# Layer 3's cross attention: the softmax weights of all heads side by side, transposed and multiplied in blocks of 128 keys

## The chip, the cores and the metric

The kernel runs on one core of a Trainium2 chip. A core has five engines that each work through a queue of their own and meet at semaphores: PE (TensorE, matrix products and transposes; PEld is its loading of weights), DVE (VectorE), ACT (ScalarE), POOL (GpSimd) and SP (SyncE, which issues most transfers). The metric is the device time of one execution in microseconds, as the median of several. All data are 32-bit floats.

## The reference

A decoder of four layers works on `x` of shape (4, 512, 128): four batches of 512 tokens of width 128. Each layer adds self attention, cross attention on a context of 77 rows, and a feed-forward. The change is in Layer 3's cross attention, which has 16 heads of 64:

```python
q = (query @ w_q).reshape(B, Q, HEADS, HEAD_DIM).transpose(0, 2, 1, 3)
k = (key @ w_k).reshape(B, Kl, HEADS, HEAD_DIM).transpose(0, 2, 1, 3)
v = (value @ w_v).reshape(B, Kl, HEADS, HEAD_DIM).transpose(0, 2, 1, 3)
scores = jnp.einsum('bhqd,bhkd->bhqk', q, k) * scale
attn = jax.nn.softmax(scores, axis=-1)
out = jnp.einsum('bhqk,bhkd->bhqd', attn, v)
out = out.transpose(0, 2, 1, 3).reshape(B, Q, HEADS * HEAD_DIM)
return out @ w_o
...
x = x + _L3_xattn_ref(_layernorm(x, axis=-1), ctx_1024, ctx_1024, L3_xattn_w_q, L3_xattn_w_k, L3_xattn_w_v, L3_xattn_w_o)
x = x + _L3_ffn_ref(_layernorm(x, axis=-1), L3_ffn_gate_w, L3_ffn_bias, L3_ffn_W1, L3_ffn_W3, L3_ffn_W2, L3_ffn_sw1, L3_ffn_sw3, L3_ffn_sw2)
```

Layer 3's feed-forward, which follows, is a mixture of 32 experts: each token goes to four of them, and each expert has a limited number of places (slots).

## The kernel before, in words

*Tiles.* P = 128 partitions, B = 4 batches, S = 512 tokens a batch, TB = 4 tiles of 128 tokens a batch, D = 128, L = 77 context rows. `xT` holds the normalised tokens as columns, `x` and `xn` hold them as rows.

*Keys and values ahead of time.* `l3_context` (woven into Layer 0's feed-forward) computes the keys of all heads and, for each head, the product of its values with its part of the output matrix: `vo` of head h has 77 rows of width 128, so that the sum over heads of weights times `vo` is already the attention's output. Both go to memory (L1999, L2012). `l3_keys` (L2015 to L2024) loads them into `kb` and `vo` ahead of Layer 3; `kb` has the two heads of a pair in a block diagonal form, so that one product gives the scores of both.

*The stage.* `l3_xattn` (L2026 to L2086) makes 32 items, four batches of eight pairs of heads, and runs four phases of each, shifted against each other: in round r stand the projection of item r, the scores of item r - 1, the products with the values of item r - 4 and the transposes of item r - 3.
- Projection: one product 128 by 512 (L417) into a bank of PSUM, copied with the scale 1/8 into `q` by ACT (L2042).
- Scores: four products (L417), two token tiles in each of two banks `s`. Then for each bank: DVE takes the maximum of each row (L516) and subtracts it into a tile `sm_e` of 4 x 77 columns (L428), ACT takes the exponential (L2059), DVE the sums and their reciprocals (L525, L526), POOL multiplies (L527). So an item has two sets of these, each 128 x 308.
- Transposes: for each of the two heads four transposes (L2068, `mm<-ident,sm_e`) of 128 tokens by 77 keys, and a copy by ACT to `eT` (L2070).
- Values: for each head one product over 77 keys (L2077, `acc<-eT,vo`) that adds into the batch's accumulator, 16 in a batch; after the last, ACT copies it to `yT` (L2083).

PSUM has eight banks: five for `mm` (projection, scores and transposes), two accumulators `acc` and one `s` for everything in the chain below.

*What is woven in.* The first 12 rounds carry the layer norms of batches 1 to 3. Rounds 12 to 19 carry a chain for batch 0, the next eight rounds one for batch 1, the remaining rounds one for batch 2, each about two and a half pieces a round. Such a chain adds the attention's output of its batch to `x` (four transposes L448 of `yT`, DVE's add L428), takes the layer norm (L475 to L508: statistics and the iterated root on DVE, the scaled rows on ACT, four transposes L507 on PE) and routes the batch (`route_slots`): gate products on PE, the four best experts by DVE (L620 to L640), the "place" products of L417 (how many tokens went to the same expert before), then `fits` (L706) and the slot numbers `to` (L737) on DVE, and last 16 scatters of 128 rows each, issued by POOL (L749). The batch's scatters need `to`; the experts need the scatters of batches 0 to 2. Batch 3 goes through a dense feed-forward later.

The program text gives the order in which the work is issued; the framework's scheduler arranges each engine's queue from it, so neighbours may change places on an engine, but each engine then works strictly through its queue. The multiplies (L527) of POOL and its scatters (L749) share one queue, as do the softmax passes and the routing on DVE.

*After the stage.* Shared rows, the experts on their slots, the gathers of their results (L860) and the dense feed-forward of batch 3 end the kernel; they have weights that POOL loads (L369).

Of the kernel before, what the change touches and what calls it, by code (L numbers as in the profile page):

```python
# [13 lines left out]
F32 = mybir.dt.float32  # L14
# [4 lines left out]
ALU = mybir.AluOpType  # L19
AX = mybir.AxisListType  # L20
PSUM = bass.MemoryType.PSUM

P = 128
B, S, D = 4, 512, 128
NT = B * S // P
TB = S // P
L = 77
# [261 lines left out]
class Net:  # L289
# [1694 lines left out]
    def l3_context(self, pool):  # L1984

        nc = self.nc
        Wk, Wv, Wo = (self.load("l3_xattn." + n, pool, "x3" + n) for n in "kvo")
        kd = self.away.tile([2, 64, 8, B, L], F32, name="x3_k")
        vd = self.away.tile([L, 16, B, D], F32, name="x3_vo")
        self.x3 = kd, vd  # L1990
        yield
        for hp in range(8):
            c = slice(hp * P, hp * P + P)
            pk = self.bank("f", (P, B, L))
            self.dot(pk.rearrange("p b l -> p (b l)"), (Wk["k"][:, c], self.const["ctxT"]))
            k = pool.tile([P, B, L], F32, tag="x3kT", name="x3kT", bufs=2)
            nc.scalar.copy(k, pk)
            for h in range(2):
                nc.sync.dma_start(kd[h, :, hp], k[64 * h : 64 * h + 64])  # L1999
            pv = self.bank("f", (P, B * L))  # L2000
            self.dot(pv, (Wv["v"][:, c], self.const["ctxT"]))
            vT = pool.tile([P, B * L], F32, tag="x3vT", name="x3vT", bufs=2)
            nc.scalar.copy(vT, pv)
            yield
            vo = pool.tile([L, 2, B, D], F32, tag="x3vo", name="x3vo", bufs=2)
            for h in range(2):
                po = self.bank("f", (P, B, D))
                r = slice(64 * h, 64 * h + 64)
                for b in range(B):
                    self.dot(po[:L, b, :], (vT[r, b * L : b * L + L], Wo["o"][r, c]))  # L2010
                nc.scalar.copy(vo[:, h], po[:L])
            nc.sync.dma_start(vd[:, 2 * hp : 2 * hp + 2], vo)  # L2012
            yield

    def l3_keys(self, pool):  # L2015

        kd, vd = self.x3
        kb = pool.tile([P, 8, B, 2, L], F32, name="kb")
        vo = pool.tile([L, 16, B, D], F32, name="vo")
        self.nc.gpsimd.memset(kb, 0.0)  # L2020
        for h in range(2):
            self.nc.sync.dma_start(kb[64 * h : 64 * h + 64, :, :, h, :], kd[h])
        self.nc.sync.dma_start(vo, vd)
        self.x3 = kb, vo  # L2024

    def l3_xattn(self, base, pool):  # L2026


        nc, tc = self.nc, self.tc
        HP = 8  # L2030
        Wq = self.pack(base, "l3_xattn.q")
        kb, vo = self.x3
        items = [(b, hp) for b in range(B) for hp in range(HP)]
        made = {}
        accs = {}

        def projections(b, hp):
            c = slice(hp * P, hp * P + P)
            pq = self.mm()
            self.dot(pq, (Wq["q"][:, c], self.tokens(b)))  # L2040
            q = pool.tile([P, S], F32, tag="q", name="q", bufs=3)
            nc.scalar.mul(q, pq, 0.125)  # L2042
            made[b, hp, "q"] = q

        def scores(b, hp):
            q = made.pop((b, hp, "q"))
            es = []
            for j0 in range(0, TB, 2):
                s = self.mm((P, 4, L))
                for j in range(2):  # L2050
                    self.dot(
                        s[:, 2 * j : 2 * j + 2, :].rearrange("p h l -> p (h l)"),
                        (q[:, (j0 + j) * P : (j0 + j + 1) * P], kb[:, hp, b].rearrange("p h l -> p (h l)")),
                    )
                es.append(s)
            made[b, hp, "e"] = []
            for s in es:
                e = self.less_maxima(s, 4, pool, 8)
                nc.scalar.activation(e, e, AF.Exp)  # L2059
                self.over_sums(e, 4, pool, 8)  # L2060
                made[b, hp, "e"].append(e)

        def turn(b, hp):
            es = made.pop((b, hp, "e"))
            for h in range(2):
                t = self.mm((P, TB, P))
                for j in range(TB):
                    nc.tensor.transpose(t[:L, j, :], es[j // 2][:, 2 * (j % 2) + h, :], self.ident)  # L2068
                eT = pool.tile([L, S], F32, tag="eT", name="eT", bufs=4)
                nc.scalar.copy(eT, t[:L].rearrange("l j q -> l (j q)"))  # L2070
                made[b, hp, h] = eT

        def values(b, hp):
            if hp == 0:
                accs[b] = self.acc()
            for h in range(2):
                nc.tensor.matmul(  # L2077
                    accs[b], lhsT=vo[:, 2 * hp + h, b, :], rhs=made.pop((b, hp, h)),
                    start=hp == 0 and h == 0, stop=hp == HP - 1 and h == 1,
                )  # L2080
            if hp == HP - 1:
                self.sums["l3_xattn", b] = pool.tile([P, S], F32, tag="yT", name="yT", bufs=2)
                nc.scalar.copy(self.sums["l3_xattn", b], accs[b])  # L2083

        return self.lagged(items, (projections, 0), (scores, 1), (values, 4), (turn, 3))

    def out(self, b):
# [206 lines left out]
```

## Time and profile before

| | |
|---|---|
| time, five runs | 2347.26, 2352.25, 2352.82, 2356.02, 2359.11 us; median 2352.82 |
| profiled execution | 2365.31 us, its span 2363.5 us |
| PE busy | 2205.5 us, 93% of the span |
| DVE, ACT, POOL busy | 1605.9 (68%), 1034.3 (44%), 571.7 us (24%) |
| first projection of the stage, last value product | near 2032 and near 2205 us |
| first scatter of batch 0, 1, 2 | 2115.55, 2160.98, 2203.32 us |
| transposes L2068, 256 of them | mean 280 ns |
| value products L2077, 128 passes | mean 594 ns |
| softmax passes on DVE, 64 sets: L516, L428, L525, L526 | mean 471, 468, 469, 171 ns |
| multiplies L527 on POOL, 64 in the stage | mean 706 ns |

The span is the time between the first and the last event of the profiled execution. In the profile's rows, L is a line of the kernel, then come the engine, the operation, the tile written and the tiles read, the shape, and how often it ran; then its busy time in us, the mean duration of one in ns, and the engine's idle time just before, with what ended it. A chain of waits is followed back from the last instruction: at each step to what released it, or to the instruction before it on its engine. Instructions overlap in their pipelines, so several of a kind take less than their number times the mean.

### The profile page before, as it was taken

How to read it: one execution, taken by the hardware profiler on the slowest of the kernel's cores; microseconds unless marked ns; L12 is line 12 of the kernel's file. 1: busy time of each engine (PE TensorE's matmuls, PEld its weight loads, DVE VectorE, ACT ScalarE, POOL GpSimd, SP SyncE). 2: the span in 40 equal slices, each digit the busy share in tenths (PEclk: the TensorE clock that was granted, in tenths of full speed). 3: DMA queues.
4: the chain of work that ended last, by engine and by line, in shares of the span. 5: the costliest groups of instructions: out<-in, count | busy, mean ns of one | idle time of the engine just before them, and what ended most of it. 6: DMA issues, size and time to landing. Idle time of an engine off the chain costs nothing.

```text
span 2363.5 us, 28673 instructions
## 1 busy us (share of the span) xinstructions
PE 2205.5 (93%) x9282; PEld 1162.0 (49%) x9282; DVE 1605.9 (68%) x4051; ACT 1034.3 (44%) x2105; POOL 571.7 (24%) x712
## 2 busy tenths in 40 slices
PE   6999899999999998999999999999999995998865
PEld 3566556644545453445444444444444443765532
DVE  6666566666676678778776787767767756776433
ACT  4555446344325553434443444444444433455410
POOL 1000001000000103333323333323333322336343
PEclk7888899999999999999999999999999997999887
DMA  5321144154453242233433334333333350000287
GB/s 160 93 64 42 44 119 123 47 142 113 114 133 94 79 130 76 74 87 94 110 85 83 96 97 109 115 80 93 101 101 91 101 134 36 1 6 1 63 164 75
DMA packets 84144, 210.95 MB, mean 89 GB/s; under 512 B 18873, under 2 KB 41721, under 8 KB 83661
## 3 DMA queue, kind: packets, MB, share of 16 engines
q1 hardware_dynamic: 79050, 198.99, 31.1%
q0 software_dynamic: 4944, 10.14, 3.5%
q8 instruction: 73, 1.20, 0.2%
q14 instruction: 77, 0.63, 0.1%
HBM read 179.76 MB, written 20.23 MB: 85 GB/s over the span
## 4 chain that ended last, share of the span: by engine, by line
PE 73%; DVE 13%; issue 5%; DMA 4%; POOL 3%; ACT 2%; SPq 0%; POOLq 0%; ACTq 0%; DVEq 0%
PE mm L417 21%; PE f L417 11%; PE mm L1783 8%; PE s L417 8%; PE acc L947 5%; PE mm L1750 5%; PE mm L1733 4%; DMA back<-made,back 2%; DVE h L428 2%; PE acc L2077 2%; PE mm L1115 1%; PE mm L1070 1%; PE mm L1137 1%; DVE m L1077 1%; PE s L507 1%
## 5 line engine op out<-in xcount | busy, mean ns | idle before, releaser
L1694 POOL TENSOR_TENSOR gvx<-gvx 128x512 f32<-128x512 f32 (+1 forms) x256 | 259.8, 1015 | 584.1 <-DVE gvx L428 528.4
L417 PE MATMUL f<-xT,w_l_ffn 128*128 128x512 f32 (+1 forms) x768 | 376.0, 611 | 11.3 <-DVE h L428 10.6
L417 PE MATMUL mm<-w_l_ffn_qkv,xT 128*128 128x512 f32 x512 | 266.3, 604 | 3.3 <-DVE roped L1665 1.7
L1814 ACT ACTIVATE at_e<-mm,at_m 128x512 f32<-128x512 f32 x256 | 172.9, 686 | 213.6 <-DVE at_m L1812 207.9
L1783 PE MATMUL mm<-og,w_l_ffn_o 128*128 128x512 f32 x512 | 264.9, 601 | 0.0
L939 ACT ACTIVATE h<-f 128x512 f32<-128x512 f32 x189 | 112.3, 596 | 292.3 <-PE f L417 265.2
L947 PE MATMUL acc<-h,w_l_ffn 128*128 128x512 f32 x378 | 201.1, 617 | 31.1 <-DVE h L428 23.3
L417 PEld LDWEIGHTS f<-xT,w_l_ffn 128*128 128x128 f32 (+1 forms) x768 | 141.6, 194 | 166.8 <-issue 130.5
L428 DVE TENSOR_TENSOR h<-h,f 128x512 f32<-128x512 f32 (+1 forms) x192 | 131.1, 684 | 130.1 <-PE f L417 102.0
L428 DVE TENSOR_TENSOR og<-mm,c 128x512 f32<-128x512 f32 x256 | 175.5, 687 | 27.3 <-PE mm L1783 26.0
L428 DVE TENSOR_TENSOR gvx<-mm,gv 128x512 f32<-128x512 f32 x256 | 174.2, 682 | 23.3 <-PE mm L417 18.9
L1734 ACT COPY eT<-mm 128x512 f32<-128x512 f32 x256 | 137.6, 595 | 73.0 <-PE mm L1733 72.8
L1812 DVE TENSOR_REDUCE at_m<-mm 128x1 f32<-128x512 f32 x256 | 161.0, 682 | 7.8 <-PE mm L417 6.1
L1733 PEld LDWEIGHTS mm<-ident,at_e 128*128 128x128 f32 x1024 | 119.6, 141 | 67.3 <-issue 49.5
L1783 PEld LDWEIGHTS mm<-og,w_l_ffn_o 128*128 128x128 f32 x512 | 89.5, 191 | 97.6 <-issue 86.1
L1733 PE MATMUL mm<-ident,at_e 128*128 128x128 f32 x1024 | 133.5, 273 | 2.6 <-ACT at_e L1814 2.6
L947 PEld LDWEIGHTS acc<-h,w_l_ffn 128*128 128x128 f32 x378 | 71.8, 196 | 126.6 <-issue 73.2
L417 PEld LDWEIGHTS mm<-w_l_ffn_qkv,xT 128*128 128x128 f32 x512 | 86.9, 190 | 92.3 <-issue 70.0
L417 PE MATMUL mm<-roped 64*128 64x512 f32 x512 | 131.7, 616 | 0.5 <-DVE gvx L428 0.4
L1077 DVE TENSOR_REDUCE m<-mm 128x1 f32<-128x512 f32 (+3 forms) x176 | 105.4, 636 | 37.3 <-PE mm L1073 36.5
L428 DVE TENSOR_TENSOR h<-h,c 128x512 f32<-128x512 f32 x176 | 121.2, 695 | 4.1 <-DMA c<-l_ffn_w 1.0
L1750 PE MATMUL mm<-eT,v 128*64 128x512 f32 x512 | 119.9, 600 | 0.0
(440 smaller groups left out, 3688.1 us busy)
## 6 DMA issues: line engine op xcount, KB each, us to landing
c<-gates SPq DMA_DIRECT2D x256, 256.0 KB
c<-l_ffn_w SPq DMA_DIRECT2D x106, 384.0 KB
w_l_ffn<-in_l_ffn SPq DMA_DIRECT2D x26, 576.0 KB
w_l_ffn_qkv<-in_l_ffn_qkv SPq DMA_DIRECT2D x16, 640.0 KB
w_l_ffn_o<-in_l_ffn_o SPq DMA_DIRECT2D x16, 512.0 KB
rot<-qk SPq DMA_DIRECT2D x128, 64.0 KB
w_l_ffn<-in_l_ffn POOLq DMA_DIRECT2D x10, 576.0 KB, 4.4
k_parts<-k SPq DMA_DIRECT2D x12, 384.0 KB
```

The lines of the kernel that those rows point to most:

```text
L417: self.nc.tensor.matmul(out, lhsT=lhsT, rhs=rhs, start=i == 0, stop=i == len(pairs) - 1)
L428: self.nc.vector.tensor_tensor(out, a, b, op)
L939: nc.scalar.activation(h, pg, AF.Silu)
L947: nc.tensor.matmul(acc["t"], lhsT=W["d" + u], rhs=h, start=i == 0, stop=i == n - 1)
L1077: nc.vector.tensor_reduce(m[:, i, h0 : h0 + per], ps, AX.X, ALU.max, negate=True)
L1694: nc.gpsimd.tensor_tensor(x[:, :, :m], x[:, :, :m], x[:, :, m : 2 * m], ALU.add)
L1733: nc.tensor.transpose(p[:, j, :], es[i][hl][:, j * P : j * P + P], self.ident)
L1734: nc.scalar.copy(eT[hl][:, :, i * P : i * P + P], p)
L1750: nc.tensor.matmul(po[64 * hl : 64 * hl + 64, :], lhsT=m["v"][:, j, hl, :], rhs=eT[hl][:, j, :], start=j == 0, stop=j == TB - 1,)
L1783: nc.tensor.matmul(acc, lhsT=W["o"][:, (e - 1) * D : e * D], rhs=hs.pop(e - 1), start=e == 1, stop=e == E)
L1812: nc.vector.tensor_reduce(m, s, AX.X, ALU.max, negate=True)
L1814: nc.scalar.activation(e[:, :n], s, AF.Exp, bias=m, accum_out=den)
```

## The change

The weights of one batch now lie in one tile `heads` of 128 tokens by 4 token tiles by 16 heads by 77 keys, two of them in turn. The subtraction of each set writes its piece (two token tiles, the two heads of the pair: 2 x 154 columns) into that tile, and exponential, sums and multiply work on the same piece. The number and the sizes of these instructions are as before. The 16 x 77 = 1232 keys of all heads are cut into blocks of 128 regardless of heads: nine full ones and one of 80. The transposes and the products with the values go by these blocks: 10 x 4 transposes and 10 products a batch instead of 16 x 4 and 16. A block is taken up with the pair of heads that completes it; the eight pairs of a batch have 1, 1, 1, 1, 2, 1, 1 and 2 blocks. The value tile is laid out to match, 128 rows by 10 blocks: `l3_context` writes its rows of (head, key) one below the other, and `l3_keys` loads nine full blocks and a rest of 80 rows in two transfers.

```diff
-        vd = self.away.tile([L, 16, B, D], F32, name="x3_vo")
+        vd = self.away.tile([16 * L, B, D], F32, name="x3_vo")
...
-            nc.sync.dma_start(vd[:, 2 * hp : 2 * hp + 2], vo)
+            nc.sync.dma_start(vd[2 * hp * L : 2 * (hp + 1) * L].rearrange("(h l) b d -> l h b d", l=L), vo)
...
-        vo = pool.tile([L, 16, B, D], F32, name="vo")
+        n, rest = 16 * L // P, 16 * L % P
+        vo = pool.tile([P, n + 1, B, D], F32, name="vo")
...
-        self.nc.sync.dma_start(vo, vd)
+        self.nc.sync.dma_start(vo[:, :n], vd[: n * P].rearrange("(r p) b d -> p r b d", p=P))
+        self.nc.sync.dma_start(vo[:rest, n], vd[n * P :])
...
+        rows = [(r, min(r + P, 16 * L)) for r in range(0, 16 * L, P)]
+
+        blocks = [[i for i, (_, r) in enumerate(rows) if (r - 1) // (2 * L) == hp] for hp in range(HP)]
...
-            made[b, hp, "e"] = []
-            for s in es:
-                e = self.less_maxima(s, 4, pool, 8)
+            if hp == 0:
+                made[b, "e"] = pool.tile([P, TB, 16, L], F32, tag="heads", name="heads", bufs=2)
+            for i, s in enumerate(es):
+                s = s.rearrange("p (j h) l -> p j h l", j=2)
+                e = made[b, "e"][:, 2 * i : 2 * i + 2, 2 * hp : 2 * hp + 2, :]
+                m, r = (pool.tile([P, 2, 2], F32, tag=t, name=t, bufs=8) for t in ("sm_m", "sm_s"))
+                wide = lambda a: a.unsqueeze(3).to_broadcast([P, 2, 2, L])
+                nc.vector.tensor_reduce(m, s, AX.X, ALU.max)
+                self.tt(e, s, wide(m), ALU.subtract)
                 nc.scalar.activation(e, e, AF.Exp)
-                self.over_sums(e, 4, pool, 8)
-                made[b, hp, "e"].append(e)
+                nc.vector.tensor_reduce(r, e, AX.X, ALU.add)
+                nc.vector.reciprocal(r, r)
+                nc.gpsimd.tensor_tensor(e, e, wide(r), ALU.mult)
 
         def turn(b, hp):
-            es = made.pop((b, hp, "e"))
-            for h in range(2):
+            e = made[b, "e"].rearrange("p j h l -> p j (h l)")
+            for i in blocks[hp]:
+                r0, r1 = rows[i]
                 t = self.mm((P, TB, P))
                 for j in range(TB):
-                    nc.tensor.transpose(t[:L, j, :], es[j // 2][:, 2 * (j % 2) + h, :], self.ident)
-                eT = pool.tile([L, S], F32, tag="eT", name="eT", bufs=4)
-                nc.scalar.copy(eT, t[:L].rearrange("l j q -> l (j q)"))
-                made[b, hp, h] = eT
+                    nc.tensor.transpose(t[: r1 - r0, j, :], e[:, j, r0:r1], self.ident)
+                eT = pool.tile([P, S], F32, tag="eT", name="eT", bufs=4)
+                nc.scalar.copy(eT[: r1 - r0], t[: r1 - r0].rearrange("l j q -> l (j q)"))
+                made[b, i] = eT
 
         def values(b, hp):
             if hp == 0:
                 accs[b] = self.acc()
-            for h in range(2):
+            for i in blocks[hp]:
+                n = rows[i][1] - rows[i][0]
                 nc.tensor.matmul(
-                    accs[b], lhsT=vo[:, 2 * hp + h, b, :], rhs=made.pop((b, hp, h)),
-                    start=hp == 0 and h == 0, stop=hp == HP - 1 and h == 1,
+                    accs[b], lhsT=vo[:n, i, b, :], rhs=made.pop((b, i))[:n], start=i == 0, stop=i == len(rows) - 1,
                 )
```

The scheduler arranges the engines' queues anew for this program, so places of unchanged instructions differ too. A weight load of the experts (L369 on POOL), which overwrites Layer 3's projection weights and so waits for PE's last projection, stood ahead of the multiplies of items 30 and 31 and now stands ahead of those of items 28 to 31. Batch 2's norm transposes (L507) stood after the transposes of item 27 and now stand after those of item 29.

## The prediction

> **What bounds the kernel now.** I first read the chain that ended last: TensorE (PE) holds most of it, and the stage's own lines are the values L2077 and part of L417.
>
> ```profile
> PE 73%; DVE 13%; issue 5%; DMA 4%; POOL 3%; ACT 2%; SPq 0%; POOLq 0%; ACTq 0%; DVEq 0%
> ```
> ```profile
> 2047.95 1.91 PE mm L417 x10
> 2049.86 1.72 PE acc L2077 x4
> 2051.58 0.88 PE mm L2068 x8
> ```
>
> The second block is the chain inside Layer 3's cross attention: a round (one pair of heads) is projection and scores 1.91, values 1.72, transposes 0.88, together 4.50 us with no gap. 32 rounds run from 2032 to 2205 us. But the windows by stage say that this bound does not last:
>
> ```profile
> core 0: us, PE busy (x) PEld busy (x) DVE busy (x) ACT busy (x) POOL busy (x), PEclk, DMA share, GB/s
> 2051.60:2060.60 9.00, 9.00 (x46) 6.04 (x45) 5.59 (x17) 5.01 (x11) 2.71 (x4) 1.00 0.01 3
> ...
> 2079.00:2115.50 36.50, 35.56 (x191) 24.89 (x190) 27.35 (x113) 22.82 (x45) 9.69 (x15) 1.00 0.00 1
> 2115.50:2161.00 45.50, 42.41 (x209) 28.58 (x208) 32.47 (x125) 25.19 (x49) 27.11 (x34) 0.96 0.03 7
> 2161.00:2203.30 42.30, 39.09 (x195) 26.02 (x193) 29.37 (x115) 22.31 (x44) 26.26 (x32) 0.96 0.06 15
> ```
>
> In steady rounds DVE has 2.79 of 4.50 us to do. From 2079 a batch's routing is woven in (27 to 32 us of DVE per batch), and from 2115.5 POOL also issues the 16 scatters of a batch. POOL's timeline shows what they do to the softmax multiplies (L527) that the transposes wait for, and PE's timeline the wait:
>
> ```profile
> 2115.55 1.30 POOL L749 DMA_INDIRECT slots<-xn,to  x1 [3.74 <-DVE to L737]
> ...
> 2137.61 0.97 POOL L749 DMA_INDIRECT slots<-xn,to  x1 [0.30 <-issue]
> 2138.60 3.98 POOL L527 TENSOR_TENSOR sm_e<-sm_e,sm_s 128x308 f32<-128x308 f32 x6
> ```
> ```profile
> 2131.70 0.44 PE L2068 MATMUL mm<-ident,sm_e 128*77 128x128 f32 x2 [1.84 <-POOL sm_e L527]
> 2132.35 1.09 PE L2068 MATMUL mm<-ident,sm_e 128*77 128x128 f32 x6 [0.21 <-POOL sm_e L527]
> 2133.23 1.91 PE L417 MATMUL mm<-xT,w_l_xattn_q 128*128 128x512 f32 x2
> ...
> 2139.37 0.44 PE L2068 MATMUL mm<-ident,sm_e 128*77 128x128 f32 x2 [0.83 <-POOL sm_e L527]
> ```
>
> I call the start of batch b's scatters Sb (S0 2115.55, S1 2160.98, S2 2203.32) and the transposes of item k Tk (T0 2041.5, T8 2079.0, T19 2140.0 and T27 2185.4 where the multiplies come free). After S2 some 160 us follow (experts, gathers, the last dense feed-forward) that the change does not touch. So the end moves as S2 moves.
>
> **The change, part by part.** The rows:
>
> ```profile
> L527 POOL TENSOR_TENSOR sm_e<-sm_e,sm_s 128x308 f32<-128x308 f32 x64 | 43.8, 706 | 70.1 <-DVE sm_s L526 38.7 <-PE mm L417 18.3 <-ACT eT L2070 7.0
> L749 POOL DMA_INDIRECT slots<-xn,to x41 | 41.1, 1002 | 23.3 <-DVE to L737 12.5 <-issue 9.2 <-PE mm L2068 0.6
> ```
> ```profile
> L2077 PE MATMUL acc<-eT,vo 77*128 77x512 f32 x128 | 60.5, 594 | 0.4 <-ACT eT L2070 0.3
> ...
> L2068 PE MATMUL mm<-ident,sm_e 128*77 128x128 f32 x256 | 35.7, 280 | 6.4 <-POOL sm_e L527 6.4
> ```
>
> *Removed.* Per batch 64 transposes become 40 and 16 products become 10. A product over 128 keys costs no more than one over 77: the 128-row product L947 has a mean of 617 ns, L2077 594 (each is issued in two passes, 128 for 64 products; four passes end 1.72 apart, so 0.86 a product). So a block of 128 keys takes 0.44 (four transposes, half of the 0.88) + 0.86 = 1.30 us, and a round 1.91 + 1.30 per block: 3.21 with one, 4.51 in the two pairs (of eight) that have two. Eight rounds: 6 x 3.21 + 2 x 4.51 = 28.3 instead of 36.0, 7.7 us of PE per batch, 31 in all. ACT loses six copies of some 0.6 us per batch; it is busy 5.01 of 9.00 us in steady rounds, so PE covers them already: nothing.
>
> *Kept.* All 64 sets of softmax instructions on DVE, ACT and POOL stay, now on pieces of two heads by 154 elements in a wider tile. I take their old times. From below, nothing can get cheaper, since the elements are the same; from above, the dearest POOL multiply of 256 elements (L1956, 868 ns against 726 at L1931) gives 19% more. DVE's widest nested pass (686 ns, weights against code) costs what a plain one of 512 elements does (684), so I stay at the lower end.
>
> *Moved.* Writing the value tile in pieces of half the size (layer 0) and loading it by one more transfer: the loads are issued near 1924 us and first needed after 2041, over 100 us of cover; nothing. Were that cover gone, the tile of 2.5 MB would cost at the 182 GB/s of its own window some 14 us. The order of each engine changes with the schedule: the third batch's norm transposes stand after T29 (before: after T27), the second batch's after the values of item 20 (before: after T19), and on POOL a weight load, which waits for the last projection, now stands ahead of the multiplies of four items instead of two.
>
> Now the stage in order, with the new order of each engine and the old durations:
> - To T0: the same work, 0.
> - T0 to T8: PE binds (DVE 8 x 2.79 = 22.3 and POOL 16 x 0.70 = 11.3 fit in 28.3): **-7.7**.
> - T8 to S0: PE from T8 to the end of the place matmuls, by the new order: 17.8 to the products of item 12, then norm 0.44, transposes 0.44, projection and gate 1.90, scores 1.05, one block 1.30, the next projection and scores 1.91, place matmuls with what stands between them 2.9: 27.7. Then DVE from fits to the slot numbers, 4.5 with the softmax passes that stand there: 32.2, against 36.1 before (2115.08 - 2079.0). Some wait for DVE, which has 27 of those 32 us to work, 0.4: **-3.5** (between -7.7, if DVE never delays, and 0).
> - S0 to T19, the burst: 16 x 1.28 (0.97 and 0.30 of issue) + 6 x 0.70 = 24.7 with its first issue 24.9, against 24.5: **+0.4**. PE gains nothing here; it waits some 10 us for T18 in place of the 3 short waits of before.
> - T19 to S1: PE 17.4 to the place matmuls (they now stand behind the scores of item 25), DVE 4.5, 0.45 to the first scatter, 1.0 because the norm's last step waits behind softmax passes: 23.4, against 21.0: **+2.4** (0 to +4).
> - S1 to T27: 24.1 against 24.4: **-0.3**.
> - T27 to S2: 0.2 to finish T27, projection, scores, products and T28 3.7, scores, two products, T29 3.2, norm and T30 with POOL's late multiplies 1.0, product 0.9, gate 1.0, T31 and last products 3.7 with their copies, place 1.7, DVE 2.6 and 0.4 of issue: 18.4, with a semaphore's 0.1 at eight handings 19.3, against 17.9: **+1.4** (0 to +4). The weight load is in this: 0.6 of issue after the last projection, then four multiplies of 0.7, ready just as PE wants them. If PE's scores did not cover it, it would cost 2.0.
> - After S2: 0.
>
> The sum is -7.3 us: the span 2363.5 becomes 2356.2. That profiled execution took 2365.31, above the five times shown (2347.26 to 2359.11), so I apply the difference to their median: 2352.82 - 7.3 = **2345.5**.
>
> The trace shows PE slow after a pause: the projection at 2133.23 took 1.91 where the steady one takes 1.02, and the window 2115.5 to 2161 has a granted clock of 0.96. The Trainium skill ("TensorE: Matmul & The Clock Gate", HAM oscillation) speaks against the change here: pauses beyond about 3.4 us drop the array to half rate. By that rule each of the two long waits would add about 1.7 us of PE time; as the bursts end by POOL, I leave it out of the sum, and with it the sum would be about -4.
>
> **The rivals.**
> 1. *PE stays the bound everywhere.* For: PE is busy 93% of the span. Against: POOL's bursts of 24.5 us and DVE's 27 to 32 us per batch. It would give 7.7 for the three batches ahead of S2, 23: 2329.7.
> 2. *All of it is given back.* Only T0 to T8 gains, the reordered chains of the three batches take it back (+0.4 + 4 + 4 - 0.3 = +8.1 against -7.7): about 2353. For: two of three chains stand later in the order; against: PE's work between has shrunk by more than the delay in the first.
> 3. *Slower: the pieces of 154 make each pass over the tile dearer.* Place: DVE's subtract and sum, POOL's multiply. At L1956's 19%, 0.18 us of DVE per tile and 0.13 of POOL: on the 48 tiles from T8 on, 48 x 0.18 = 8.6, and 6 multiplies in each of three bursts or tails 18 x 0.13 = 2.4: 11.0 - 7.3 = +3.7: 2356.5. It decides from 13% dearer. Against it stands DVE's nested pass at a plain price.
>
> **How the numbers follow.** A measurement of this kernel tells 0.3%, 7.1 us, from no change. Forecast 0.60: its own range is -13 to -2, so 0.31 faster, 0.27 same, 0.02 slower. Rival 1 0.09 (faster). Rival 2 0.16 (0.13 same, 0.03 slower). Rival 3 0.15 (0.14 slower, 0.01 same). Faster 0.40, same 0.41, slower 0.19. The low end takes the best of each bound (-15.3) and 2.5 of spread: 2335; the high end takes in rival 3: 2358.
>
> **What will show it.** 160 transposes near 280 ns and 80 passes of products near 600 ns; T8 near 2071, S0 near 2104, S1 near 2153, S2 near 2196 if the stage starts at the same time; PE's wait for POOL at the transposes grown from 6 to some 20 us; DVE near full from 2071 to 2104. I am wrong if S0 comes after 2110, if the multiply is over 0.8 us, or if S2 - T27 is over 22.

## The result, and the profile after

The changed kernel takes 2347.74 us (median of 33 runs, 2342.89 to 2354.41), the kernel before 2355.19 us (median of 59 runs): a ratio of 0.9969, with a 95% interval of 0.9960 to 0.9977. That is 7.4 us less; 7.3 had been forecast. The sum was right, its parts were not all: the stage itself gave less, 4.6 to 5.3 us, and that the totals agree to 0.1 us is luck.

I read the marks of the prediction from PE's, DVE's and POOL's timelines, in us from the stage's first projection, in the two profiled executions of each kernel (the second ones are among the experiments):

| | before | before again | after | after again |
|---|---|---|---|---|
| first projection, from the span's start | 2032.3 | 2022.5 | 2019.4 | 2027.8 |
| end of T8 | 47.6 | 47.6 | 39.0 | 39.7 |
| S0, first scatter of batch 0 | 83.3 | 83.3 | 71.1 | 71.7 |
| end of T19 | 108.6 | 108.6 | 97.0 | 96.6 |
| S1 | 128.7 | 128.7 | 120.2 | 119.8 |
| end of T27 | 154.0 | 154.0 | 144.3 | 143.9 |
| S2 | 171.0 | 171.1 | 166.5 | 165.7 |
| from S2 to the end | 160.2 | 164.8 | 161.7 | 163.1 |

From the first projection to S2 the marks repeat within 0.1 us (before) and 0.8 us (after), and the change is worth 4.6 to 5.3 us there. Where the stage starts differs by 10 us between executions of one and the same kernel, and so does the stretch behind S2 by 4.6: comparing the two first profiles as wholes (2363.5 against 2347.6 us) would have shown 15.9 us, 12.9 of them ahead of the first changed instruction of the stage.

The groups of the stage in the changed kernel, POOL's and PE's (busy us, mean ns of one, then the idle time just before and its causes):

```profile
L2075 POOL TENSOR_TENSOR heads<-heads,sm_s 128x308 f32<-128x308 f32 x64 | 44.9, 711 | 69.3 <-DVE sm_s L2074 36.7 <-PE mm L417 17.9 <-ACT heads L2072 3.8
```
```profile
L2093 PE MATMUL acc<-eT,vo 128*128 128x512 f32 (+1 forms) x80 | 41.1, 612 | 0.6 <-ACT eT L2085 0.6
...
L2083 PE MATMUL mm<-ident,heads 128*128 128x128 f32 (+1 forms) x160 | 26.2, 285 | 22.3 <-POOL heads L2075 22.3
```

The products fell from 60.5 to 41.1 us and the transposes from 35.7 to 26.2, 28.9 us of PE gone, where 31 had been counted; the mean of each is nearly the old one (612 against 594, 285 against 280). The multiply on pieces of the wide tile takes 711 ns against 706. But PE's wait for it has grown from 6.4 to 22.3 us. Where, the windows say: they run from the first projection to the end of T8, to S0, to S1 and to S2.

```profile
core 0: us, PE busy (x) PEld busy (x) DVE busy (x) ACT busy (x) POOL busy (x), PEclk, DMA share, GB/s
2019.40:2058.40 39.00, 38.80 (x186) 26.36 (x187) 30.68 (x100) 26.30 (x58) 13.91 (x20) 0.95 0.00 1
2058.40:2090.50 32.10, 31.35 (x172) 22.49 (x170) 26.58 (x113) 20.77 (x42) 9.77 (x16) 1.00 0.01 2
2090.50:2139.60 49.10, 38.11 (x180) 25.45 (x179) 32.67 (x128) 22.38 (x45) 28.47 (x34) 0.86 0.02 6
2139.60:2185.90 46.30, 33.25 (x143) 21.15 (x142) 27.71 (x113) 17.88 (x36) 25.82 (x32) 0.83 0.05 14
```

Up to S0 PE is full, 38.8 of 39.0 and 31.4 of 32.1 us. In the two stretches with scatters PE is busy 38.1 of 49.1 and 33.3 of 46.3 us, although a lower granted clock (PEclk, the share of PE's full clock) of 0.86 and 0.83 makes its work longer; the stretch from S0 to S1 has grown from 45.4 to 49.1. POOL's timeline in the first burst, and PE's beside it:

```profile
2095.88 1.01 POOL L749 DMA_INDIRECT slots<-xn,to  x1 [0.17 <-issue]
2097.19 0.97 POOL L749 DMA_INDIRECT slots<-xn,to  x1 [0.30 <-issue]
...
2103.57 0.97 POOL L749 DMA_INDIRECT slots<-xn,to  x1 [0.30 <-issue]
2104.55 0.72 POOL L2075 TENSOR_TENSOR heads<-heads,sm_s 128x308 f32<-128x308 f32 x1
...
2109.01 0.71 POOL L2075 TENSOR_TENSOR heads<-heads,sm_s 128x308 f32<-128x308 f32 x1
```
```profile
2105.33 0.69 PE L2083 MATMUL mm<-ident,heads 128*128 128x128 f32 x2 [5.91 <-POOL heads L2075]
2109.78 0.69 PE L2083 MATMUL mm<-ident,heads 128*128 128x128 f32 x2 [3.76 <-POOL heads L2075]
2110.26 1.92 PE L417 MATMUL mm<-xT,w_l_xattn_q 128*128 128x512 f32 x2
2111.97 2.26 PE L417 MATMUL mm<-kb,q 128*128 128x154 f32 x8
```

Seven scatters stand in a row ahead of the first multiply of item 18 and three more ahead of the second; each half of T18 starts as its multiply ends. After these waits the projection takes 1.92 us where it takes 1.02 in steady rounds.

### The profile page after: what moved, and what is told of

It reads as the page before. It is cut to its first block, busy times and chain, and to the rows that moved or that the text cites. A ratio compares the mean times of both kernels' runs of the same rounds, so it can differ in the third digit from the quotient of the medians.

```text
span 2347.6 us, 28317 instructions
## 1 busy us (share of the span) xinstructions
PE 2168.4 (92%) x9138; PEld 1136.6 (48%) x9138; DVE 1601.1 (68%) x4051; ACT 1018.6 (43%) x2080; POOL 572.2 (24%) x712
## 4 chain that ended last, share of the span: by engine, by line
PE 72%; DVE 13%; issue 5%; DMA 4%; POOL 3%; ACT 2%; SPq 0%; POOLq 0%; DVEq 0%; ACTq 0%
PE mm L417 21%; PE f L417 11%; PE mm L1783 8%; PE s L417 7%; PE acc L947 5%; PE mm L1750 5%; PE mm L1733 4%; DMA back<-made,back 2%; DVE h L428 2%; PE mm L1070 1%; PE mm L1137 1%; PE mm L1115 1%; POOL slots L749 1%; DVE m L1077 1%; DVE k_work L428 1%
## 5 line engine op out<-in xcount | busy, mean ns | idle before, releaser
L947 PE MATMUL acc<-h,w_l_ffn 128*128 128x512 f32 x378 | 200.7, 616 | 31.4 <-DVE h L428 23.3
```

The lines of the kernel that those rows point to most:

```text
L947: nc.tensor.matmul(acc["t"], lhsT=W["d" + u], rhs=h, start=i == 0, stop=i == n - 1)
```

## The experiments

### The two kernels again

Both unchanged, for a second trace of each.

> The kernel before, unchanged, once more, for a second trace. Between the two profiled executions at hand the first projection of Layer 3's cross attention already comes 12.9 us earlier in the changed kernel, with no changed instruction ahead of it but the writing of the value tile in layer 0. Theory A (the spread of executions, in layer 0's first 250 us): this trace shows another start of the stage, several us from 2032.3, while the stretch from the first projection to the first scatter of batch 2 stays at 171.0 us within 1, and from there to the end at 160.2 within 3. Theory B (the change itself made the earlier layers faster): the stage starts at 2032 within 2 here.

> The changed kernel, unchanged, once more. Theory A (spread): the stage starts anywhere from 2018 to 2033 us; from its first projection to the first scatter of batch 2 166.5 us within 1, from there to the end 161.8 within 3. Theory B: the stage starts at 2019 within 2, as in the first trace of it.

They took 2360.03 and 2358.38 us, one execution each; the marks are in the table. The stage starts at 2022.5 and 2027.8, so the 12.9 us between the first two profiles were the spread of executions (theory A); theory B has neither start. The stretch behind S2 differed by 4.6 us in the kernel before, more than the 3 I had allowed, and by 1.4 in the changed one.

### Without the scatters

In both kernels:

```diff
-            for k in range(K):
+            for k in range(0):
 
                 put = nc.gpsimd.indirect_dma_start(
```

> The changed kernel without the 48 scatters of rows to the experts' slots (the slots stay empty, the experts work on zeros). Theory A (the scatters on POOL's queue hold back the multiplies, so PE's saving is lost there): from the first projection to the slot numbers of batch 2 it falls from 166 to 140 to 148 us, the transposes of items 17 to 19 and 25 to 27 follow each other at 3.2 to 4.5 us, and against the kernel before without scatters it is 12 to 20 us faster in this stretch, where with them it is 4.6. Theory B (the longer routing chain and DVE hold it back, not the scatters): it falls by no more than both kernels do, to some 158, and the gain over the kernel before without scatters stays at 3 to 7 us.

> The kernel before without the 48 scatters of rows to the experts' slots (slots empty). Theory A: PE waited only some 6 us in each of two bursts, so the stretch from the first projection to the slot numbers of batch 2 falls from 171 to about 160 us (32 rounds less the last, 4.5 each, and 3 x 3.2 of routing products, some 155, with small waits). Theory B: the same, 158 to 163.

The slot numbers of batch 2 come at 137.3 us in the changed kernel and at 161.4 us in the kernel before: 24.2 us apart, where with scatters they are 4.6 to 5.3 apart. One execution each took 2314.78 and 2341.22 us, 26.4 apart. This is theory A, and beyond its 12 to 20 us and its 140 to 148: the whole of PE's saving for the three batches ahead of the slot numbers, 3 x 7.7 = 23.1, is there. The windows of the changed kernel without scatters, in the same four stretches:

```profile
2023.60:2063.00 39.40, 39.20 (x186) 26.75 (x187) 30.70 (x99) 26.35 (x58) 13.94 (x20) 0.94 0.00 1
2063.00:2094.60 31.60, 30.85 (x170) 22.24 (x169) 26.08 (x112) 20.73 (x42) 9.73 (x15) 1.00 0.01 2
2094.60:2129.30 34.70, 34.25 (x180) 23.55 (x179) 32.20 (x128) 21.76 (x44) 12.22 (x18) 1.00 0.00 1
2129.30:2160.80 31.50, 28.71 (x146) 18.58 (x144) 27.71 (x112) 18.77 (x37) 10.02 (x16) 1.00 0.18 55
```

The third stretch takes 34.7 instead of 49.1 us, PE is full in it at a granted clock of 1.00, and DVE does the same 32 us of work within it. So neither DVE nor the longer chain held the changed kernel in that stretch: the scatters did.

### Scatters spread out

The scatters become a generator of their own with a yield after each, and that of batch 0 is woven in beside batch 1's routing (in both kernels):

```diff
-        net.weave(some(steps, 8), chain5(1), 0.41)
-        net.weave(steps, chain5(2), 0.41)
+        net.weave(some(steps, 8), net.turns(chain5(1), net.scatters(0)), 0.25)
+        net.weave(steps, chained(net.turns(chain5(2), net.scatters(1)), net.scatters(2)), 0.25)
```

> The changed kernel with the scatters of batch 0 issued one by one beside the routing of batch 1, and those of batch 1 beside the routing of batch 2, instead of in one go after each routing. Theory A (a burst of 16 scatters of 1.28 us holds back the multiplies that PE's transposes wait for): POOL has some 4 us to do in a round of 3.5 to 4.5, the pauses of 6 and 4 us ahead of the transposes of items 18 and 26 shrink to under 3, the slot numbers of batch 2 come 140 to 152 us after the stage's first projection instead of 166, and the kernel gets 10 to 25 us faster than the one before, where the change alone gives 7. Theory B (the longer chain of routing on DVE and the order set the pace): the slot numbers of batch 2 stay at 160 to 168, the gain stays at 5 to 9 us.

> The kernel before with the same spreading of the scatters. Theory A: its PE has 4.5 us to do in each round, so it gains only the pauses of the two bursts, 6 to 10 us: the slot numbers of batch 2 at 161 to 165 us after the stage's first projection instead of 170.6; the changed kernel with spreading is then 10 to 18 us ahead of it. Theory B: the two differ by 5 to 9 us, as they do without spreading.

The changed kernel with spreading has a ratio to the kernel before of 0.9956 (0.9936 to 0.9976), its slot numbers of batch 2 at 162.2 us; the kernel before with spreading 1.0014 (1.0003 to 1.0026), at 171.9. Both slot numbers miss A's (140 to 152 and 161 to 165), and the first lies in B's 160 to 168; by the medians, 2348.96 and 2360.80 us, the two kernels are 11.8 us apart, inside A's 10 to 18. But the edit didn't do what it was meant to. POOL's timeline in the changed kernel with spreading:

```profile
2101.89 0.97 POOL L754 DMA_INDIRECT slots<-xn,to  x1 [0.30 <-issue]
2103.16 0.97 POOL L754 DMA_INDIRECT slots<-xn,to  x1 [0.30 <-issue]
...
2108.26 0.97 POOL L754 DMA_INDIRECT slots<-xn,to  x1 [0.30 <-issue]
2109.24 0.72 POOL L2080 TENSOR_TENSOR heads<-heads,sm_s 128x308 f32<-128x308 f32 x1
```

The scheduler still put seven scatters in a row (one at 2100.58 and these six) ahead of item 18's multiply, and from S0 to S1 it takes 49.3 us, as without spreading. The experiment tells nothing between the theories; that the text's order alone doesn't set the queue's order is what it shows.

### Multiplies on DVE

The changed kernel with some of the multiplies given to DVE, first those between the scatters, then all that PE can reach during a burst:

```diff
-                nc.gpsimd.tensor_tensor(e, e, wide(r), ALU.mult)
+                by = nc.vector if b * HP + hp in (17, 18, 19, 25, 26, 27) else nc.gpsimd
+                by.tensor_tensor(e, e, wide(r), ALU.mult)
```

> The changed kernel with the softmax multiplies of items 17 to 19 and 25 to 27, which stand between the scatters on POOL's queue, given to DVE (12 of 0.47 us). Theory A: the transposes of items 17 to 19 and 25 to 27 no longer wait for POOL; those of items 20 and 28 come after the burst, 22 us after its start, where now 29.5 and 28; the slot numbers of batch 2 at 148 to 158 us, 8 to 18 us less than in the changed kernel. Theory B (DVE is the bound there): DVE's 5.6 us come on top, the slot numbers stay at 164 to 172 us.

> The same with the multiplies of items 17 to 22 and 25 to 30 on DVE, all that PE can reach in 20 us of scatters. Theory A: PE runs through the bursts; DVE has 22.3 + 7.5 + 5.6 = 35 us to do per batch against PE's 31.5, so DVE becomes the bound with 35 us per batch: the slot numbers of batch 2 at 142 to 152 us. Theory B: 166 or later, since DVE was the bound already.

With items 17 to 19 and 25 to 27: ratio 0.9929 (0.9911 to 0.9948), the slot numbers at 155.5 us, T17, T18 and T19 at 75.4, 79.1 and 82.3 us, one round after another, and the end of T20 at 94.8, 23.8 after S0 (22 expected). The scatters are all still issued here, so it was their place in POOL's queue ahead of the multiplies, and not their transfers, that held T17 to T19. With items 17 to 22 and 25 to 30: **2330.04 us, ratio 0.9879 (0.9861 to 0.9897)**, the slot numbers at 142.6 us, inside the 142 to 152 expected. Its windows, from S0 to S1 and from S1 to S2:

```profile
2091.80:2128.10 36.30, 33.70 (x179) 23.39 (x178) 35.03 (x140) 22.11 (x44) 19.41 (x22) 1.00 0.03 8
2128.10:2163.50 35.40, 30.35 (x134) 19.96 (x133) 30.33 (x123) 17.41 (x35) 19.10 (x21) 0.88 0.07 18
```

The third stretch is down from 49.1 to 36.3 us, and DVE is now busy 35.0 of it, so DVE has hardly a gap there; in the fourth it is busy 30.3 of 35.4. This version beats both kernels, by 29 us the one before.

### The same on the kernel before, a filled wait, and two more places for the multiplies

These four ran together, on another chip than the runs above. The edits: the same twelve items on DVE in the kernel before; transposes that nobody reads, ahead of T18 and T26 in the changed kernel; item 31 added to the twelve; all 64 on DVE.

```diff
+            if b * HP + hp in (18, 26):
+                t = self.mm((P, TB, P))
+                for j in range(72):
+                    nc.tensor.transpose(t[:, j % TB, :], self.ident, self.ident)
             for i in blocks[hp]:
```

> The kernel before with the softmax multiplies of items 17 to 22 and 25 to 30 on DVE, as in the changed kernel that ran at 142.6 us from its first projection to the slot numbers of batch 2. Theory A (the scatters on POOL's queue hide the change's saving): without that hold PE is the bound of the kernel before, 4.5 us a round, so it comes to 160 to 164 us as it did without scatters (161.4), a gain of 7 to 11 us over the kernel before; the change is then worth 17 to 21 us between the two kernels with these multiplies on DVE. Theory B (giving the multiplies to DVE helps both alike, by 24 us): 146 to 150 us.

> The changed kernel with 72 transposes of the identity, read by nobody, ahead of the transposes of items 18 and 26, 7.9 us in a wait of PE of about 10 us. Theory A (PE runs at half rate for some 3.4 us after such a pause, and the projection of 1.9 us and the scores of 2.2 us that follow it lie on the way to the next slot numbers): with the filling they take 1.0 and 1.2 us, item 19's transposes end 3.4 to 4 us after item 18's instead of 4.8 and 5.9, and the slot numbers of batch 2 come 161 to 164 us after the first projection instead of 165.3 and 166.0. Theory B (the slower work is hidden, or the filling delays the transposes): 165 to 168 us.

> The changed kernel with the multiplies of items 17 to 22 and 25 to 31 on DVE: item 31's too, whose transposes ended 8.6 us after those of item 30 while its multiplies stood on POOL behind a weight load and DVE's routing. If POOL's place was what held item 31, the slot numbers of batch 2 come 1 to 3 us earlier than the 142.6 us of the version with items 17 to 22 and 25 to 30; if DVE's work holds it, at 142 to 144 us.

> The changed kernel with all 64 multiplies on DVE. DVE then has 22.3 + 7.5 us of softmax and some 10 of routing to do per batch, 40 us, against PE's 31.5. If DVE is then the bound, the first eight rounds take 31 us instead of 29 and the slot numbers of batch 2 come at 148 to 160 us, later than with items 17 to 22 and 25 to 30 alone (142.6) and still earlier than in the changed kernel (166). If DVE hides it all, 141 to 144 us.

| | ratio to the kernel before | slot numbers of batch 2 |
|---|---|---|
| before, 12 items on DVE | 1.0053 (1.0030 to 1.0075) | 180.7 us |
| after, filled waits | 0.9954 (0.9937 to 0.9971) | 159.9 us |
| after, 13 items on DVE | 0.9947 (0.9926 to 0.9967) | 159.5 us |
| after, all on DVE | 0.9979 (0.9963 to 0.9995) | 163.4 us |

All four slot numbers are outside every expectation written for them. Their traces have pauses during the first two bursts of scatters that none of the ten others shows there. ACT's timeline of the version with 13 items:

```profile
2103.28 0.60 ACT L2049 ACTIVATE q<-mm 128x512 f32<-128x512 f32 x1
2111.62 0.59 ACT L2086 COPY eT<-mm 128x512 f32<-128x512 f32 x1 [7.74 <-remote]
```

ACT stands still for 7.7 us although the transposes it copies were done at 2105.6; "remote" means that the trace finds the end of the wait in nothing the core's engines did. PE and DVE stop behind it, 6.7 and 5.5 us. There are three such pauses in that trace (18.6 us in all), three in the one with all on DVE (18.6), one of 7.2 in the filled one, and in the kernel before with multiplies on DVE T18 and T27 each come 12.8 us after the transposes ahead of them, where 4.5 is a round: 16.6 us lost, without which it would be at 164, the upper end of A's 160 to 164. That subtraction is an argument, not a measurement, and the runs of these kernels spread far more (2339 to 2352 us for 13 items, against 2329 to 2331 for 12). What the pauses are, and whether they belong to these programs or to that chip, stays open; no run of the version with 12 items was made there. So what the change is worth between two kernels with the multiplies on DVE is not settled, nor what all 64 on DVE cost in the bursts. Ahead of its first pause that version reaches S0 at 74.5 us, about 3 later than the changed kernel. Item 31 can be read behind the pauses: from the end of T30 to the slot numbers both versions, with 12 and with 13 items, take 10.1 us, and in both T31 stands on PE's queue behind place products. So POOL's place did not hold item 31.

The filled wait can still be read. PE's timeline after the first filling and after the second:

```profile
2114.79 1.40 PE L417 MATMUL mm<-xT,w_l_xattn_q 128*128 128x512 f32 x2
2116.03 1.21 PE L417 MATMUL mm<-kb,q 128*128 128x154 f32 x8
...
2156.42 0.86 PE L2087 MATMUL mm<-ident,heads 128*128 128x128 f32 x4
2157.12 1.02 PE L417 MATMUL mm<-xT,w_l_xattn_q 128*128 128x512 f32 x2
2157.98 1.60 PE L417 MATMUL mm<-kb,q 128*128 128x154 f32 x8
```

In the changed kernel projection and scores took 1.92 and 2.26 after the first wait, 1.91 and 2.26 after the second. Item 19's transposes end 3.9 us after item 18's (5.9 and 4.8 in the changed kernel). So these long waits of PE do bring the half rate, and filling them avoids most of it (theory A). But the 6 us by which S2 came earlier (160.3) are not all from that: the scheduler also put batch 1's norm transposes back to just after T19 and batch 2's to just after T27, where they stand in the kernel before. From T19 to S1 this kernel takes 20.0 us against 23.2, and from T27 to S2 15.3 against 22.2 and 21.8, although the projection behind T27 ran at half rate here (1.92 us, after a wait of 3.31). Order and clock were changed together in this run; the other traces part them for the last stretch, as shown below.

## Why the prediction was right

**The rows.** Blocks of 128 keys cost nearly what those of 77 did, the pieces of two heads cost DVE and POOL nothing (462, 465, 467 ns for the three long passes of DVE against 471, 468, 469; 711 against 706 on POOL). Rival 3 needed 13% and falls.

**Step by step,** forecast against the two traces of after (differences to before, from ends of transposes):

| | forecast | measured |
|---|---|---|
| T0 to T8 | -7.7 | -8.0, -7.9 |
| T8 to S0 | -3.5 | -3.6, -3.6 |
| S0 to T19 | +0.4 | +0.6, -0.5 |
| T19 to S1 | +2.4 | +3.1, +3.1 |
| S1 to T27 | -0.3 | -1.2, -1.2 |
| T27 to S2 | +1.4 | +5.2, +4.8 |
| to S2, from the first projection | -7.3 | -4.6, -5.3 |

The main reason held and was shown by taking it away: the burst of scatters, not PE, sets the time from S0 on, and with the scatters gone the change is worth the 24 us that rival 1 counted on. PE's wait for T18 was forecast at 10 us and is 5.91 + 3.76 = 9.7. DVE was not near full before S0, though I had said it would be: 26.6 of 32.1 us.

**The step that failed is T27 to S2.** From the point where T27's multiplies come free, S2 is 22.6 and 22.2 us away in the two traces, where I had 19.3 (17.9 before). With that one of the prediction's own signs of being wrong, S2 - T27 over 22, came in. The term most under its size in both traces is "norm and T30 with POOL's late multiplies": 1.0 in the sum, some 2.4 and 2.7 on PE's timeline. "T31 and last products" took 4.3 in both instead of 3.7.

The queues of ACT and DVE show why the norm is late. Its last step on DVE is L481; in the changed kernel (first trace), and then in the kernel before:

```profile
2163.74 0.58 ACT L2085 COPY eT<-mm 128x512 f32<-128x512 f32 x1 [4.39 <-PE mm L2083]
2165.97 0.45 ACT L2072 ACTIVATE heads<-heads 128x308 f32<-128x308 f32 x1
2166.52 0.47 DVE L2073 TENSOR_REDUCE sm_s<-heads 128x4 f32<-128x308 f32 x1 [4.60 <-ACT heads L2072]
2171.74 0.14 DVE L481 SCALAR_TENSOR_TENSOR nmr<-mv,rstd 128x4 f32<-128x4 f32 x1
```
```profile
2181.88 0.15 DVE L481 SCALAR_TENSOR_TENSOR nmr<-mv,rstd 128x4 f32<-128x4 f32 x1
```

In the kernel before, L481 starts 3.5 us ahead of the point where T27's multiplies come free. In the changed kernel the steps of the norm's root stand on DVE behind and between softmax passes; the first of these waits for an exponential that stands on ACT behind T27's copy. So L481 starts 8.5 us behind that point, and 7.7 in the second trace: the third chain can hardly begin before the burst has let T27 go. The changed kernel without scatters has the chain at the same place (L481 starts 8.0 us behind T27's second half), no burst and a granted clock of 1.00, and still takes 21.9 us from there to the slot numbers; the filled kernel, where L481 stands ahead of T27, takes 16.0 from there to S2. No run moves this chain alone, so its price is read from traces of kernels that differ in more.

The half rate of PE, which I had left out "as the bursts end by POOL", did not make this miss. Behind T27 in the first and in the second trace of after:

```profile
2163.54 1.84 PE L417 MATMUL mm<-xT,w_l_xattn_q 128*128 128x512 f32 x2
2165.18 2.12 PE L417 MATMUL mm<-kb,q 128*128 128x154 f32 x8
```
```profile
2171.53 1.02 PE L417 MATMUL mm<-xT,w_l_xattn_q 128*128 128x512 f32 x2
2172.39 1.21 PE L417 MATMUL mm<-kb,q 128*128 128x154 f32 x8
```

The first trace is 1.7 us slower in these two, and its whole stretch is longer by 0.3 only. By the rule of the Trainium skill ("TensorE: Matmul & The Clock Gate", HAM oscillation) I had put the sum at about -4, and the stage gave -4.6 and -5.3; that this is nearer than -7.3 is luck, as the trace without the half rate behind T27 missed by nearly as much. Nor do these traces show the rule's bound on the length of a pause: in the kernel before, waits of 1.84 and 1.80 us were followed by projections of 1.91 and 1.80 us, while in the second trace of after one of 2.38 us was followed by 1.02.

**The total** of -7.4 (5.4 to 9.4 by its interval) holds the forecast; the stage's own 4.6 to 5.3 lies just below that interval. With the parts outside the stage spreading by 5 to 10 us per execution, the traces can't say where the other 2 us are, or that they are anything but spread. Rival 2, all given back, is out: T8 to S0 kept its gain.

## What to carry to other kernels

Before counting an engine's saving, look at what else stands in the queue of the engine that feeds it: here 16 scatters of 1.28 us between multiplies of 0.7 took 20 of a burst's 25 us. The remedy was neither on PE nor in the scatters but in moving twelve items' multiplies to an engine with time to spare. Whether that pays as much without the first change is not settled here. And mark a stage by its own events, from its first instruction, in two executions of each kernel, before laying a difference of whole spans to an edit.

## What was not expected of the hardware

- ACT stood still for up to 8.3 us at a time during the first two bursts of scatters in four traces taken together, and the trace finds the end of these waits in nothing the core's engines did. In the second traces of the two kernels such a pause stands in the third burst only (ACT 10.0 us in the changed kernel, DVE 2.2 in the one before), in the other eight there is none in the stage or the burst behind it. All such pauses of more than 2.4 us begin within a burst of scatters.
- PE's unread transposes did not run in one go either: ahead of T18 47 ran in 5.40 us, and the rest in small groups with gaps of 0.3 to 1.0 us laid to "issue", so that 72 of them took 13.8 us instead of 7.9 and T18 ended 2 to 3 us later. Ahead of T26 the 72 took 9.8 us.
- A half-rate PE appears after shorter waits too: in the version with 12 items on DVE, after waits of 0.65, 0.49 and 1.30 us within 4 us, most of the place products took 0.61 us a pair in place of 0.39.
